# One tile and four fetches for the turned probabilities of a turn, keys fetched whole, and the residual's load behind the stores of q and k

## The chip, the cores and the metric

One NeuronCore of a Trainium2 chip runs the whole program. The metric is the device time of one execution in microseconds (us). The engines are TensorE (PE), VectorE (DVE), ScalarE (ACT), GpSimd (POOL) and SyncE (SP); each works through its own instructions in order, and semaphores hold an instruction back until what it reads or overwrites is ready. In this kernel SP issues every DMA.

## What is computed

Two layers of masked attention over 128 graphs of 128 nodes with 512 features each, in float32. Layer 0 has 4 heads, layer 1 has 8; each layer adds its output to its input and normalises.

```python
# layer 0: x (128, 128, 512), adj (128, 128, 128) of True and False
q, k, v = heads(x @ Wq), heads(x @ Wk), heads(x @ Wv)            # 4 heads of 64
attn = softmax(where(adj, q @ k.T * scale, -max))
x = layernorm(x + (attn @ v) @ Wo + bo)
# layer 1
h = layernorm(x) * gamma + beta
q, k, v = split(h @ w_qkv.T, 3)                                  # 8 heads of 64
attn = softmax(where(adj | eye, q @ k.T * scale, -1e9))
x = layernorm(x + (attn @ v) @ w_out.T + b_out)
```

## The kernel before

The 128 graphs go in 64 groups of 2. A loop of steps `step(s)` runs over the groups as a software pipeline: in step s the first layer's projections of group s are made, its scores and softmax for group s-1, its attention for group s-2, and of the second layer the q, k and v products of group s-3, the scores and softmax of s-4 and the attention and output of s-5. `opening`, `closing` and `last` fill and empty the pipeline. The order of all instructions is written out by hand in these functions; nothing reorders it. The matrix products use a seven-product scheme for 2 by 2 blocks (numbers 1 to 7 in the calls).

Softmax work of a step comes in three parts: part 0 is layer 0 (2 graphs of 4 heads), parts 1 and 2 are the two graphs of layer 1 (8 heads each). Each part is a tile of 128 by 1024 float32, 512 KB. `masked` fills it from the scores, `maxima`, `exps` and `normalised` make probabilities, with the last multiplication on POOL.

Several tensors have to be transposed over 128 partitions. VectorE transposes blocks of 32 by 32, and a trip through DRAM puts the blocks in place: `put` (or a direct store) writes the turned tile to a DRAM scratch, and `fetch` (L216 to L220) reads it back in four DMAs, one for each quarter of 32 partitions. These trips are:

- probabilities: `blocks` turns a part into `turnedp` (L604) and stores it to `scrp` (L214); `probs_arrive` fetches it into `pT`. There is one tile and one scratch per part, so 3 stores of 512 KB and 12 fetches of 128 KB in a step. `attend` of the next step multiplies with `pT` (L650).
- keys and queries of layer 1: `taken_tokens` adds up a product and turns it into `tk` or `tq` (L381), each in two halves, one per graph. Keys are stored by halves (L384, 256 KB each) and fetched by halves (`k_arrive`, 4 DMAs of 64 KB each); queries are stored once (L386, 512 KB) and fetched into `rawq` (`q_arrive`, 4 DMAs of 128 KB). `q_in_order` scales them into `qo` on ScalarE (L412). Scores of the next step read `kt` and `qo` (L536).
- the inputs of the two layers: `turn` and `arrive` (`turned`, `scr`, `raw0` and `raw`), one store of 512 KB and 4 fetches of 128 KB each.

The residual of a group is loaded a second time by `load_rows` (L80) into one of five buffers `r`, which the store of an earlier group's output (L719, in `norms`, called by `flush`) has to have left. The bias is added to it on POOL (`addend`, L671) before the output products are summed into it on VectorE (L502).

On SP, a step issues in this order: the next group's `x` and mask, `raw`, the output's store, the residual's load, the stores of part 0, of `turned`, and of part 1, the fetches of part 0, one half of the keys' store, the store of part 2, `raw0`, the fetches of part 1, the stores of q and of the other half of k, the first half of the keys' fetches, the fetches of part 2, the store of layer 1's `turned`, the q fetches, and the other half of the keys' fetches. Two `turned` buffers serve all five turns through DRAM of probabilities and inputs, so a turn waits for the store before the last.

Of the kernel before, what the change touches and what calls it, by code (L numbers as in the profile page):

```python
# [10 lines left out]
F32 = mybir.dt.float32  # L11
# [6 lines left out]
P = 128  # L18
# [9 lines left out]
def kernel(ctx: ExitStack, tc: tile.TileContext, x, adj, wq, wk, wv, wo, bo,  # L28
# [96 lines left out]

    w1 = const.tile([P, KC, 3 * INNER[1]], F32, name="w1")
    wo1 = const.tile([P, INNER[1] // P, E], F32, name="wo1")
    gb_raw = one.tile([2 * KC, P], F32, tag="pT1", name="gb_raw")
    gb = const.tile([P, 2 * KC], F32, name="gb")

    setup = []
# [79 lines left out]
    def put(t, name):  # L211

        scr = dram.tile(list(t.shape), F32, tag=name.split("_")[0], name=name)
        nc.sync.dma_start(scr, t)  # L214
        return scr

    def fetch(dst, scr):
        src = scr.rearrange("(a r) q x -> r q a x", r=32)
        for q in range(4):
            nc.sync.dma_start(dst[32 * q:32 * q + 32], src[:, q])  # L220
# [167 lines left out]
    def k_tile(g):  # L388
        KT[g] = one.tile([P, 4, G, K1, 32], F32, tag="kt", name=f"kt_{g}")
        return KT[g]  # L390
# [8 lines left out]
            RAW["q"] = one.tile([P, 4, G, K1, 32], F32, tag="raw", name=f"rawq_{g}")  # L399
            fetch(RAW["q"].rearrange("p a b c j -> p a (b c j)"), SCRQ["q"].rearrange("p q b x -> p q (b x)"))  # L400

    def k_arrive(g, b):

        if 0 <= g < NG and g not in PLAIN_QK:
            kt = KT[g] if b else k_tile(g)
            fetch(kt[:, :, b].rearrange("p a c j -> p a (c j)"), SCRQ["k"][:, :, b])

    def q_in_order(g):

# [67 lines left out]
    def out_product(l, g, *which):  # L477
        if not 0 <= g < NG:
            return
        aT = AT[l, g]  # L480
        hk = INNER[l] // P // 2
        w, ws = WO[l], WSO[l]
        EH = E // 2
        for i in which:
            sums_at = {3: 3, 5: 0, 6: 1, 7: 2}
            left = (SO[l, g][:, sums_at[i]] if i in sums_at else
                    {1: aT[:, 0, :hk], 2: aT[:, 0, hk:], 4: aT[:, 1, hk:]}[i])
            right = {1: w[:, :hk, :EH], 2: w[:, hk:, :EH], 3: w[:, hk:, EH:], 4: ws[:, 2],
                     5: w[:, :hk, EH:], 6: ws[:, 0], 7: ws[:, 1]}[i]
            bank, first = INTO[i]  # L490
            if first and bank == "c":
                ACC["o", bank] = mm_tile(f"oc{l}_{g}")
            elif first:
                ACC["o", bank] = ps_st.tile([P, 512], F32, tag=(bank, f"{bank}0")[l == 1 or g >= NG - 2],
                                          name=f"o{bank}{l}_{g}")
            acc = ACC["o", bank][:, :EH]
            for c in range(hk):
                nc.tensor.matmul(acc, left[:, c], right[:, c], start=first and c == 0, stop=c == hk - 1,  # L498
                                 skip_group_check=True)
            b, h = {1: (0, 0), 2: (0, 0), 6: (0, 1), 3: (0, 1), 5: (1, 1), 7: (1, 1), 4: (1, 0)}[i]  # L500
            part = R[g][:, b, h * EH:(h + 1) * EH]
            nc.vector.tensor_add(part, acc, part)  # L502
# [7 lines left out]
    def group_of(s, part):  # L510
        g = s - (4 if part else 1)
        return g if 0 <= g < NG else None
# [70 lines left out]
    def normalised(s, *parts):  # L583
        for part in parts:
            if group_of(s, part) is None:
# [3 lines left out]
            nc.gpsimd.tensor_tensor(SM[part], SM[part], rec[:, :, :, None].to_broadcast([P, 2, K1, N]),  # L589
                                    op=ALU.mult)  # L590

    def turned_tile(s, part):

        pT = PT[group_of(s, part), part] = one.tile([P, 4, 2 * K1, 32], F32, tag=f"pT{part}",
                                                    name=f"pT{part}_{s}")
        return pT

    def blocks(s, *parts):


        for part in parts:
            if group_of(s, part) is not None:
                t = one.tile([P, 4, 2 * K1 * 32], F32, tag="turned", bufs=2, name=f"turnedp{part}_{s}")
                nc.vector.transpose(t.rearrange("p q (h r) -> p q h r", r=32),  # L604
                                    SM.pop(part).rearrange("p i k (q r) -> p q (i k) r", r=32))
                SCR["p", part] = put(t, f"scrp{part}_{s}")

    def probs_arrive(s, *parts):
        for part in parts:
            if group_of(s, part) is not None:  # L610
                fetch(turned_tile(s, part).rearrange("p a h i -> p a (h i)"), SCR.pop(("p", part)))

    def blocks_direct(s, *parts):

# [196 lines left out]
    def step(s):  # L811

        made = scores(s)
        load_ahead(s + 1)
        if s > 2:
            in_order(s)
            sums(0, s)
        arrive(1, s - 3)
        masked(made, s, 0, 1, 2)
        attend(s)  # L820
        maxima(s, 0, 1)
        out_sums(0, s - 2)
        exps(s, 0, 0)
        product_0(s, 1)
        exps(s, 0, 1)
        out_product(0, s - 2, 1, 2, 5)
        maxima(s, 2)
        product_0(s, 2)
        normalised(s, 0)
        out_product(0, s - 2, 6, 3)  # L830
        exps(s, 1, 0)
        stats(1, s - 6, 0)
        stats(1, s - 6, 1)
        product_0(s, 6)
        exps(s, 1, 1)
        out_product(0, s - 2, 7)
        product_0(s, 5)
        out_product(0, s - 2, 4)
        flush()
        load_rows(s - 1)  # L840
        normalised(s, 1)
        finish(s - 3, 0)
        stats(0, s - 2, 0)
        stats(0, s - 2, 1)
        exps(s, 2, 0)
        blocks(s, 0)
        product_0(s, 7)
        finish(s - 3, 1)
        exps(s, 2, 1)
        product_0(s, 3)  # L850
        turn(0, s + 1)
        normalised(s, 2)
        product_0(s, 4)
        if s in (2, 3):
            prepare(len(setup) - (s == 2))
        blocks(s, 1)
        probs_arrive(s, 0)
        qk(s - 3, 1)
        if s == 2:
            weight_sums(w1qk, wsqk, 1)  # L860
            prepare(1)
        flush()
        qk(s - 3, 2)
        blocks(s, 2)
        arrive(0, s + 1)
        probs_arrive(s, 1)
        qk(s - 3, 6, 5)
        flush(latest)
        addend(1, s - 5)
        out_sums(1, s - 5)  # L870
        qk(s - 3, 7, 3, 4)
        k_arrive(s - 3, 0)
        probs_arrive(s, 2)
        turn(1, s - 2)
        out_product(1, s - 5, 1, 2)
        q_arrive(s - 3)
        v(s - 3, 1, 2)
        k_arrive(s - 3, 1)
        cleared(s + 1, 0, 1, 2)
        with_self(s - 2)  # L880
        out_product(1, s - 5, 6)
        v(s - 3, 6, 5)
        out_product(1, s - 5, 5)
        v(s - 3, 7, 3)
        out_product(1, s - 5, 7)
        q_in_order(s - 3)
        v(s - 3, 4)
        out_product(1, s - 5, 3, 4)
        addend(0, s - 1)
        if s == 2:  # L890
            weight_sums(w1v, wsv, 0, 1)
        if s == 3:
            weight_sums_out(1)

    def closing(s):

        made = scores(s)
        arrive(1, s - 3)
        masked(made, s, 0, 1, 2)
        attend(s)  # L900
        maxima(s, 0, 1)
        finish(s - 3, 0)
        out_sums(0, s - 2)
        if s == NG:
            stats(1, s - 6, 0)
            stats(1, s - 6, 1)
        exps(s, 0, 0)
        out_product(0, s - 2, 1, 2, 5)
        maxima(s, 2)
        flush()  # L910
        load_rows(s - 1)
        finish(s - 3, 1)
        qk(s - 3, 1)
        exps(s, 0, 1)
        out_product(0, s - 2, 6, 3)
        qk(s - 3, 2)
        normalised(s, 0)
        exps(s, 1, 0)
        out_product(0, s - 2, 7, 4)
        stats(0, s - 2, 0)  # L920
        stats(0, s - 2, 1)
        qk(s - 3, 6)
        exps(s, 1, 1)
        addend(1, s - 5)
        out_sums(1, s - 5)
        qk(s - 3, 5)
        normalised(s, 1)
        exps(s, 2, 0)
        blocks(s, 0)
        flush()  # L930
        qk(s - 3, 7)
        exps(s, 2, 1)
        turn(1, s - 2)
        blocks(s, 1)
        probs_arrive(s, 0)
        qk(s - 3, 3)
        normalised(s, 2)
        flush(latest)
        cleared(s + 1, 0, 1)
        qk(s - 3, 4)  # L940
        probs_arrive(s, 1)
        out_product(1, s - 5, 1, 2)
        k_arrive(s - 3, 0)
        q_arrive(s - 3)
        k_arrive(s - 3, 1)
        blocks(s, 2)
        if s < NG + 2:
            v(s - 3, 1)
        out_product(1, s - 5, 6, 5)
        if s < NG + 2:  # L950
            v(s - 3, 2, 6, 5)
        out_product(1, s - 5, 7)
        probs_arrive(s, 2)
        out_product(1, s - 5, 3, 4)
        q_in_order(s - 3)
        if s < NG + 2:
            v(s - 3, 7, 3, 4)
        stats(1, s - 5, 0)
        stats(1, s - 5, 1)
        cleared(s + 1, 2)  # L960
        addend(0, s - 1)
        with_self(s - 2)
# [78 lines left out]
```

## Time and profile before

| | |
|---|---|
| three runs | 3250.31, 3254.69, 3259.03 us; median 3254.69 |
| the profiled execution | 3262.01 us, with a span of 3260.2 us; granted TensorE clock 0.944 on average |
| DMA packets | 482,790, 570.93 MB, 175 GB/s on average |
| DMA engines | 59.8% of the span in packets of the queue that SP issues to |
| chain that ended last | PE 59%, DMA 17%, SP's queue 8%, DVE 7% of the span |

The span runs from the first to the last instruction on the chip; the time of an execution is a little longer. In the rows of the profile an instruction is named by its engine, its line in the kernel, its operation and the tiles it writes and reads (`out<-in`). PEld is the loading of weights into TensorE beside its products. "SPq" is SP's queue of DMA issues. The granted clock is the share of full speed that TensorE was allowed. The transfers that matter here, with their sizes and the median time from issue to landing:

```profile
scrp<-turnedp SPq DMA_DIRECT2D x189, 512.0 KB, 4.4
pT<-scrp SPq DMA_DIRECT2D x756, 128.0 KB, 3.8
r<-in_x_dram SPq DMA_DIRECT2D x63, 512.0 KB, 4.1
scrk<-tk SPq DMA_DIRECT2D x124, 256.0 KB, 3.6
scrq<-tq SPq DMA_DIRECT2D x62, 512.0 KB, 4.8
kt<-scrk SPq DMA_DIRECT2D x496, 64.0 KB, 3.7
rawq<-scrq SPq DMA_DIRECT2D x248, 128.0 KB, 4.1
```

### The profile page before, as it was taken

What the parts mean: (1) busy time and instruction counts of PE and PEld (TensorE: products, weight loads), DVE (VectorE), ACT (ScalarE), POOL (GpSimd) and SP (SyncE); (2) the same over time, 40 slices, a digit from 0 to 9 for tenths busy, and PEclk for the clock granted to TensorE, in tenths of its full rate; (3) what the DMA queues carried; (4) which work ended last, traced back from release to release, by engine and by line L of the source; (5) the groups of instructions that cost most, each with busy time, mean ns of one, the idle gap of its engine ahead of it and who ended that gap; (6) DMA issues with size and microseconds to landing.
All of it is one profiled execution on the core that took longest, in us unless ns stands there. A gap on an engine that the chain in (4) does not pass through costs nothing.

```text
span 3260.2 us, 54135 instructions
## 1 busy us (share of the span) xinstructions
PE 2918.0 (90%) x18077; PEld 2306.4 (71%) x18077; DVE 1931.4 (59%) x3545; ACT 1536.9 (47%) x4871; POOL 1744.8 (54%) x2311
## 2 busy tenths in 40 slices
PE   8899998898898988989899889889898998898987
PEld 8667767777677777676777767767777777677766
DVE  6566555566565555655656556556555566565554
ACT  3445445355454453544544535445445455354443
POOL 4455555564555555545556555555555564554553
PEclk9999999999999999999999999999999999999999
DMA  5565665655756656556566575565665665756642
GB/s 164 176 202 158 179 191 166 195 172 167 212 154 179 197 160 195 166 166 201 162 188 186 160 206 169 169 204 158 184 194 163 195 181 159 212 159 173 188 124 71
DMA packets 482790, 570.93 MB, mean 175 GB/s; under 512 B 60872, under 2 KB 383440, under 8 KB 482512
## 3 DMA queue, kind: packets, MB, share of 16 engines
q1 hardware_dynamic: 482512, 567.46, 59.8%
q8 instruction: 145, 2.38, 0.3%
q14 instruction: 133, 1.09, 0.1%
HBM read 304.09 MB, written 263.19 MB: 174 GB/s over the span
## 4 chain that ended last, share of the span: by engine, by line
PE 59%; DMA 17%; SPq 8%; DVE 7%; issue 5%; POOL 2%; ACT 2%; DVEq 0%; ACTq 0%; POOLq 0%
PE qka L338 10%; PE a L460 8%; DMA rawq<-scrq 7%; SPq L220 7%; PE av L650 6%; PE oa L498 6%; PE qkf L338 5%; PE sc L536 3%; PE va L338 3%; DMA scrp<-turnedp 3%; PE sc_a L536 3%; PE qkc L338 3%; PE of L498 3%; PE c L460 2%; PE f L460 2%
## 5 line engine op out<-in xcount | busy, mean ns | idle before, releaser
L302 POOL TENSOR_TENSOR xs<-xT 128x256 f32<-128x256 f32 x256 | 186.4, 728 | 835.9 <-ACT xT L256 695.0
L580 ACT ACTIVATE sm<-sm,nmax 128x128 f32<-128x128 f32 x1536 | 594.3, 391 | 5.5 <-DVE nmax L571 5.5
L589 POOL TENSOR_TENSOR sm<-sm,rec 128x1024 f32<-128x1024 f32 x192 | 364.1, 1896 | 279.6 <-DVE rec L588 273.7
L671 POOL TENSOR_TENSOR r<-r,bias 128x1024 f32<-128x1024 f32 x128 | 301.3, 2354 | 147.2 <-ACT r L670 147.2
L604 DVE STREAM_TRANSPOSE turnedp<-sm 128x1024 f32<-128x1024 f32 x189 | 231.7, 1226 | 200.9 <-DMA scrp<-turnedp 129.2
L412 ACT ACTIVATE qo<-rawq 128x512 f32<-128x512 f32 x124 | 71.2, 621 | 592.4 <-DMA rawq<-scrq 592.4
L502 DVE TENSOR_TENSOR r<-oa,r 128x256 f32<-128x256 f32 x508 | 207.9, 409 | 240.4 <-PE oa L498 123.3
L536 PE MATMUL sc_a<-kt,qo 64*128 64x128 f32 x512 | 125.2, 418 | 227.5 <-ACT qo L412 226.5
L580 ACT ACTIVATION_READ_ACCUMULATOR sm<-sm,nmax 128x1 f32 x1536 | 291.2, 190 | 0.0
L347 ACT COPY ev<-va 128x256 f32<-128x256 f32 x128 | 47.6, 372 | 512.1 <-PE va L338 512.1
L536 PEld LDWEIGHTS sc_a<-kt,qo 64*128 64x128 f32 x512 | 107.1, 307 | 240.0 <-ACT qo L412 238.6
L502 DVE TENSOR_TENSOR r<-of,r 128x256 f32<-128x256 f32 x254 | 107.3, 423 | 216.6 <-PE of L498 209.9
L338 PE MATMUL qkf<-w,xs 128*128 128x512 f32 x496 | 233.2, 592 | 0.5 <-ACT eqk L347 0.5
L338 PE MATMUL qka<-wsqk,xs 128*128 128x512 f32 x496 | 233.1, 592 | 0.0
L571 DVE TENSOR_REDUCE nmax<-sm 128x8 f32<-128x1024 f32 x192 | 226.4, 1205 | 0.2
L498 PE MATMUL oa<-wso,so 128*128 128x256 f32 x760 | 208.6, 384 | 11.0 <-DVE r L502 6.3
L565 DVE COPY_PREDICATED sm<-m,sc 128x512 f32<-128x512 uint8 x256 | 171.5, 723 | 64.6 <-PE sc L531 45.3
L498 PE MATMUL of<-wo,so 128*128 128x256 f32 x760 | 208.3, 383 | 0.8 <-POOL so L302 0.7
L565 DVE COPY_PREDICATED sm<-m,sc_a 128x512 f32<-128x512 uint8 x64 | 46.8, 732 | 267.4 <-PE sc_f L536 254.2
L716 ACT ACTIVATE r<-r,shift,root 128x512 f32<-128x512 f32 x254 | 193.0, 808 | 23.4 <-POOL shift L705 23.4
L302 POOL TENSOR_TENSOR so<-aT 128x256 f32<-128x256 f32 (+1 forms) x254 | 150.2, 591 | 75.5 <-ACT aT L653 75.5
L338 PEld LDWEIGHTS qkf<-w,xs 128*128 128x128 f32 x496 | 94.2, 190 | 119.5 <-issue 117.7
(178 smaller groups left out, 7300.0 us busy)
## 6 DMA issues: line engine op xcount, KB each, us to landing
scrp<-turnedp SPq DMA_DIRECT2D x189, 512.0 KB, 4.4
pT<-scrp SPq DMA_DIRECT2D x756, 128.0 KB, 3.8
scr<-turned SPq DMA_DIRECT2D x125, 512.0 KB, 4.2
raw<-scr SPq DMA_DIRECT2D x500, 128.0 KB, 3.8
r<-in_x_dram SPq DMA_DIRECT2D x63, 512.0 KB, 4.1
out_dram<-r SPq DMA_DIRECT2D x63, 512.0 KB, 2.8
scrk<-tk SPq DMA_DIRECT2D x124, 256.0 KB, 3.6
scrq<-tq SPq DMA_DIRECT2D x62, 512.0 KB, 4.8
```

Of the source, the lines that this page charges most:

```text
L220: nc.sync.dma_start(dst[32 * q:32 * q + 32], src[:, q])
L302: nc.gpsimd.tensor_tensor(o, a0, a1, op=op)
L338: nc.tensor.matmul(o, lhsT, rhs, start=first and m == 0, stop=m == len(todo) - 1, skip_group_check=True)
L460: nc.tensor.matmul(acc[:, at * P:(at + 1) * P], lhsT, rhs, start=first and n == 0, stop=n == len(todo) - 1, skip_group_check=True)
L498: nc.tensor.matmul(acc, left[:, c], right[:, c], start=first and c == 0, stop=c == hk - 1, skip_group_check=True)
L502: nc.vector.tensor_add(part, acc, part)
L536: nc.tensor.matmul(ps[h % 2][:, h // 2, :].rearrange("p (a j) -> p a j", j=32), QO[g, b][r, h // 2], keys_of(g, b, h // 2, r), start=True, ...
L571: nc.vector.tensor_reduce(NMAX[part], SM[part], AX.X, ALU.max, negate=True)
L580: nc.scalar.activation(sm[:, i, k, :], sm[:, i, k, :], AF.Exp, bias=nmax[:, i, k:k + 1], accum_out=total[:, i, k:k + 1])
L589: nc.gpsimd.tensor_tensor(SM[part], SM[part], rec[:, :, :, None].to_broadcast([P, 2, K1, N]), op=ALU.mult)
L604: nc.vector.transpose(t.rearrange("p q (h r) -> p q h r", r=32), SM.pop(part).rearrange("p i k (q r) -> p q (i k) r", r=32))
L671: nc.gpsimd.tensor_tensor(R[g], R[g], (bias0, bias1)[l][:, None, :].to_broadcast([P, G, E]), op=ALU.add)
```

## The change

The three parts of a step share one `pT` tile and one DRAM scratch, in which the 3 parts of a row's quarter lie side by side. Each part is still stored on its own; all that a step has are fetched together in four DMAs of up to 384 KB. The keys are fetched whole, in four DMAs of 128 KB behind the q fetches, instead of by halves. In `step`, the store of part 0 is put ahead of the output's store, and the residual's load behind the stores of q and k; the normalisation of part 2 moves behind the turn of part 1. In `closing`, all probabilities are fetched at the place where part 2's were. A small setup tile takes another tile's buffer, since `pT1` is gone.

```diff
-    gb_raw = one.tile([2 * KC, P], F32, tag="pT1", name="gb_raw")
+    gb_raw = one.tile([2 * KC, P], F32, tag="sm2", name="gb_raw")
...
-    def k_arrive(g, b):
+    def k_arrive(g):
 
         if 0 <= g < NG and g not in PLAIN_QK:
-            kt = KT[g] if b else k_tile(g)
-            fetch(kt[:, :, b].rearrange("p a c j -> p a (c j)"), SCRQ["k"][:, :, b])
+            fetch(k_tile(g).rearrange("p a b c j -> p a (b c j)"), SCRQ["k"].rearrange("p q b x -> p q (b x)"))
...
+    PALL, SCRP = {}, {}
+
     def turned_tile(s, part):
 
-        pT = PT[group_of(s, part), part] = one.tile([P, 4, 2 * K1, 32], F32, tag=f"pT{part}",
-                                                    name=f"pT{part}_{s}")
+        if s not in PALL:
+            PALL[s] = one.tile([P, 4, 3, 2 * K1, 32], F32, tag="pT", name=f"pT_{s}")
+        pT = PT[group_of(s, part), part] = PALL[s][:, :, part]
         return pT
...
-                SCR["p", part] = put(t, f"scrp{part}_{s}")
+                if s not in SCRP:
+                    SCRP[s] = dram.tile([P, 4, 3, 2 * K1 * 32], F32, tag="scrp", name=f"scrp_{s}")
+                nc.sync.dma_start(SCRP[s][:, :, part], t)
 
     def probs_arrive(s, *parts):
-        for part in parts:
-            if group_of(s, part) is not None:
-                fetch(turned_tile(s, part).rearrange("p a h i -> p a (h i)"), SCR.pop(("p", part)))
+        parts = [p for p in parts if group_of(s, p) is not None]
+        if parts:
+            for part in parts:
+                turned_tile(s, part)
+            lo, hi = parts[0], parts[-1] + 1
+            fetch(PALL[s][:, :, lo:hi].rearrange("p a t h i -> p a (t h i)"),
+                  SCRP[s][:, :, lo:hi].rearrange("p q t x -> p q (t x)"))
...
@@ step(s)
         out_product(0, s - 2, 4)
+        normalised(s, 1)
+        blocks(s, 0)
         flush()
-        load_rows(s - 1)
-        normalised(s, 1)
         finish(s - 3, 0)
...
-        blocks(s, 0)
         product_0(s, 7)
...
-        normalised(s, 2)
         product_0(s, 4)
...
         blocks(s, 1)
-        probs_arrive(s, 0)
+        normalised(s, 2)
         qk(s - 3, 1)
...
         arrive(0, s + 1)
-        probs_arrive(s, 1)
         qk(s - 3, 6, 5)
...
         qk(s - 3, 7, 3, 4)
-        k_arrive(s - 3, 0)
-        probs_arrive(s, 2)
+        load_rows(s - 1)
+        probs_arrive(s, 0, 1, 2)
         turn(1, s - 2)
         out_product(1, s - 5, 1, 2)
         q_arrive(s - 3)
         v(s - 3, 1, 2)
-        k_arrive(s - 3, 1)
+        k_arrive(s - 3)
...
@@ closing(s)
         blocks(s, 1)
-        probs_arrive(s, 0)
...
-        probs_arrive(s, 1)
         out_product(1, s - 5, 1, 2)
-        k_arrive(s - 3, 0)
         q_arrive(s - 3)
-        k_arrive(s - 3, 1)
+        k_arrive(s - 3)
         blocks(s, 2)
...
-        probs_arrive(s, 2)
+        probs_arrive(s, 0, 1, 2)
         out_product(1, s - 5, 3, 4)
```

## The prediction

> **What bounds the kernel now.** I read the totals first, then the list of who TensorE (PE) waited for, then one step of the SP queue in order of time, then short windows with the transfer rate.
>
> ```profile
> span 3260.2 us, 54135 instructions
> PE 2918.0 (90%) x18077; PEld 2306.4 (71%) x18077; DVE 1931.4 (59%) x3545; ACT 1536.9 (47%) x4871; POOL 1744.8 (54%) x2311
> ```
>
> ```profile
> PE sc_a L536 <- ACT qo L412: 226.5, 59, 5.1
> PE a L460 <- DVE qkv L474: 68.8, 62, 1.5
> PE av L650 <- DMA pT<-scrp: 8.2, 4, 3.0
> ```
>
> PE is busy 90% of the span, and of the 342 us that it idles, 226.5 lie in one place, once per step (59 times, 3.84 us each): the first layer-1 score product of a step waits for the scaled queries qo (us in total, times, longest). A step is about 50 us. The 68.8 us at L460 wait for VectorE sums whose order the change leaves as it was. So only the qo wait can move much. Its release, in the SP queue (start, duration, engine, line, operation):
>
> ```profile
> 1634.31 1.80 SPq L220 DMA_DIRECT2D pT<-scrp  x4
> 1636.21 0.38 SPq L386 DMA_DIRECT2D scrq<-tq  x1
> 1636.71 0.52 SPq L384 DMA_DIRECT2D scrk<-tk  x1
> 1637.27 3.21 SPq L220 DMA_DIRECT2D kt<-scrk  x4
> 1640.59 2.01 SPq L220 DMA_DIRECT2D pT<-scrp  x4
> 1642.70 0.37 SPq L214 DMA_DIRECT2D scr<-turned  x1
> 1643.17 2.19 SPq L220 DMA_DIRECT2D rawq<-scrq  x4
> 1645.41 2.09 SPq L220 DMA_DIRECT2D kt<-scrk  x4
> ```
>
> and beside it what VectorE (DVE) and PE did, from their own orders of time:
>
> ```profile
> 1632.51 0.71 DVE L381 STREAM_TRANSPOSE tq<-eqk 128x512 f32<-128x512 f32 x1
> ```
>
> ```profile
> 1645.48 1.16 PE L531 MATMUL sc<-qkv 64*128 64x128 f32 x16
> 1650.31 0.58 PE L536 MATMUL sc_a<-kt,qo 64*128 64x128 f32 x1 [3.67 <-ACT qo L412]
> ```
>
> The turned queries tq are ready at 1633.22, but their store is issued only at 1636.21, because SP is still issuing older fetches. The last q fetch starts at 1644.89, lands near 1649.5, ACT scales (0.64), PE starts at 1650.31: **17.1 us after tq is ready**. PE has run out of other work at 1646.64, **13.4 us** after tq. The wait is the difference, and the forecast needs one number: what becomes of 17.1.
>
> The rates decide that (window, its length, busy time and count of PE, PEld, DVE, ACT, POOL, granted clock, DMA share, GB/s):
>
> ```profile
> 5.00:8.00 3.00, 2.46 (x11) 1.94 (x10) 0.69 (x1) 0.83 (x2) 1.60 (x3) 1.00 1.08 295
> 21.00:25.00 4.00, 4.00 (x43) 3.71 (x41) 2.82 (x4) 1.36 (x3) 2.30 (x4) 1.00 1.05 399
> 1625.00:1626.50 1.50, 1.50 (x5) 0.64 (x4) 0.12 (x1) 0.47 (x1) 1.50 (x1) 1.00 1.02 418
> 1635.00:1638.00 3.00, 3.00 (x15) 2.64 (x14) 2.08 (x6) 0.37 (x1) 3.00 (x4) 1.00 1.05 224
> 1607.00:1617.00 10.00, 10.00 (x82) 9.47 (x79) 6.42 (x17) 8.61 (x38) 4.54 (x9) 1.00 0.00 0
> ```
>
> All but the last are at a DMA share of about 1, so the DMA engines are full in each. Loads into all 128 partitions run at 399 GB/s (2 KB pieces) and 295 (weights, 512 B pieces); stores from 128 partitions at 418; but the fetches, each into 32 partitions in 1 KB pieces, at 224. Small pieces alone do not explain that, since 512 B pieces reach 295. Two more fetch windows give 233 (3184.5 to 3187) and 236 (1646 to 1649); the best single microsecond is 273. Meanwhile, early in the step (1607 to 1617), nothing moves at all.
>
> **The change, part by part.** *Removed:* 8 of the 12 pT issues and 4 of the 8 kt issues per step, about 0.45 us each on SP, so 5.4 us of SP time. Without them SP reaches the q store in time: its last work before is the raw0 fetch, issued as soon as scr0 has landed and scrp2 is stored, about 1628 to 1631. The q store then goes at 1633.3 instead of 1636.2. That is 2.9 us won.
>
> *Moved into the tail:* the same bytes of pT now all lie between the k store and the q fetch: before, 4 fetches of 128 KB were there, now 4 of 384 KB, 1.57 MB in all. The residual's load (512 KB) is there too, and k's whole fetch is behind q's, where PE needs all of it for the first two products. Counting landings from the issue of the q store (each transfer after the first costs its bytes by its rate, since they queue):
> - q store, alone: 2.61 and 3.08 are what scrp stores took from issue to landing where nothing else ran (chain of waits at 3208.95 and 3139.42); 2.85.
> - k store, 262 KB at 295 (the 512 B row): 0.89. Residual, 524 KB at 399: 1.31.
> - pT, 1,573 KB at 224: **7.02**.
> - scr1 store, 524 KB at 418: 1.25.
> - q fetch, 524 KB at 224: 2.34; k fetch, the same: 2.34.
>
> Sum 18.0 us, where 17.1 stood. q is there at 15.7 and scaled by 16.4, so k's landing takes the place of q as what ends the wait. SP doesn't bound this: 16 issues at 0.47 are 7.5 us, and even where an issue waits for the transfer eight before it to land (the built program asks that), the last k fetch goes when scr1 has landed, at 13.3, and needs some 3 us. PE's wait grows by 0.9 us a step.
>
> *The rate is the unshown term.* No row has a 384 KB fetch in 3 KB pieces. Bounds: 399 as the wide loads (pT 3.94, sum 14.9) and 216, the slowest fetch window (1598 to 1600; pT 7.28, q and k 2.43 each, sum 18.4). I take 224, since destination (32 partitions), source and queue are those of the fetch rows and only the piece grows. The residual's load can cost more than its share: alone it lands 4.1 us after its issue, 0.6 later than the sum has it. With a first store of 3.08 and the slowest rate that makes 19.3, so +2.2 at the upper end.
>
> The Trainium skill speaks on both sides here. "DMA: Bandwidth & Descriptors", rules for kernel authors, says to merge many small transfers into a large one; that would put pT nearer 399 and the sum near 14.9. "SBUF — State Buffer", the DMA port swizzle, says that partitions 0 to 31 reach only 8 of 16 ports, measured there as 189 GB/s at 1 MiB with a limit of 218, whatever the piece; by 218 the sum would be 18.3. The 224 of this trace, half of 418, agrees with the second.
>
> *Parts at nothing.* The scrp stores become 512 pieces of 1 KB instead of 128 of 4 KB: between 1.25 us (418) and 1.78 (295) each, in the stretch from 1618 to 1630, where the DMA share is 0.29 to 1.06, 0.64 on average; that slack covers it, 0.5 us each without it. turnedp0 goes ahead of two statistics on DVE (1.23 us later); the POOL chain of 1.56 us behind them then starts at 1619.4 instead of 1618.7 and ends at 1621.0, before POOL's next work at 1621.75. The out store has scrp0 ahead of it on SP; nobody waits for it but the residual, which moves later. Residual: lands about 5 to 6 us after tq, 1638.3 to 1639; the bias add on POOL (1638.27, 2.35 us) waits up to 1 us, and POOL is idle from 1640.6 to the next step. pT lands 12.1 us after tq, 6 us ahead of its use. The reciprocal behind turnedp1 still waits for ACT until 1623.2. gb_raw's other place: used once, at the start.
>
> *Clock.* After each wait PE runs at a lower granted clock: the same products take 6.3 to 7.8 us at a granted clock of 0.60 to 0.75 (1500.7 to 1508.5, 1601 to 1607.5), and 4.9 at 1.00 in the step at 3095.5, the one with no wait. Longer waits fall among the 7.6 to 7.8 more often: half the steps by 0.6 us, +0.3 a step.
>
> *Sum.* (0.91 + 0.3) x 58 steps = 70. The step that ends at 3095.5 has no wait now (its q store left SP at once, 13.3 us before): it would get 4.7 plus about 2 of clock, +7. In the closing steps all probabilities now arrive in the last place: 4.7, 2.3 and 2.3 us more fetching at three places where PE already waits for pT (5.6 us); I take 6 of these 9. Together **+83 us**. The profiled execution took 3262.01 us (span 3260.2), so 3345; the median of the runs is 7.3 lower, so 3338.
>
> **Rivals.**
> 1. *pT runs at the wide rate.* For it: bigger pieces, less per piece. Against: 224 in 1 KB pieces beside 295 in 512 B pieces. Sum 14.9, -2.2 a step, and up to 1 us of clock: 13 - 2.2 x 58 is -115, with clock -173; 3080 to 3140, 3110. It decides from 6.1 us for pT (258 GB/s) downward: below that the kernel is faster.
> 2. *Between:* pieces of 3 KB help some, 240 to 290 GB/s; pT 6.6 to 5.4, the step moves +0.4 to -0.9 us; 3210 to 3285, no change in the middle.
> 3. *Worse:* the residual's latency and the slow rate both count, +2.2 and 0.4 of clock: 3254.7 + 13 + 150 = 3418.
> 4. *Nothing moves,* as bytes are the same and only issues fall: then 3255. Against: PE's wait is fed by the very tail whose order changes.
>
> **How the numbers follow.** Forecast 0.70 (own range 3285 to 3395), rival 1 0.14, 2 and 4 together 0.11, 3 0.05. A measurement of this kernel tells 0.3% (10 us) from no change. Slower: 0.70 and 0.05, less 0.04 at the forecast's lower edge, plus 0.02 of the cases between, 0.73. The 0.13 that is left beside rival 1 gives 0.05 to no change and 0.08 to faster, 0.22 with rival 1. The range leaves out most of rival 1 and of 3: 3180 to 3395.
>
> **What would show it.** SP issues scrq within 0.5 us of tq's end; pT takes 9 us and more from issue to landing; fetch windows stay at 215 to 240 GB/s; PE's wait at L536 is put down to kt<-scrk, not to qo, with 270 to 300 us over 60 places. Wrong if windows of pT alone show over 260 GB/s, or if the wait shrinks.

## The result, and the profile after

| | before | after |
|---|---|---|
| median of the runs | 3254.02 us (3250.31 to 3259.03) | 3428.91 us (3424.05 to 3431.28) |
| ratio | | 1.0535, 95% interval 1.0516 to 1.0553 |
| span of the profiled execution | 3260.2 us | 3427.0 us |
| granted TensorE clock, mean | 0.944 | 0.922 |

The kernel became slower, as forecast, but by 175 us where 83 were forecast; 3429 lies outside the range (3180 to 3395) and next to rival 3 (3418). The list of who PE waited for, after (us in total, times, longest):

```profile
PE sc_a L535 <- ACT qo L411: 292.1, 54, 10.0
PE a L459 <- DVE qkv L473: 68.9, 62, 1.5
PE sc_a L535 <- DMA kt<-scrk: 41.0, 7, 7.0
PE sc_f L535 <- DMA kt<-scrk: 24.0, 60, 0.9
PE av L658 <- DMA pT<-scrp: 12.9, 2, 6.6
```

The wait at the first layer-1 score product (L535, L536 before) has grown from 226.5 to 333 us, and a new one of 24 us has come to the product after it, sc_f. One step of the SP queue after:

```profile
1665.64 0.34 SPq L386 DMA_DIRECT2D scrq<-tq  x1
1666.64 0.52 SPq L384 DMA_DIRECT2D scrk<-tk  x1
1667.21 0.65 SPq L80 DMA_DIRECT2D r<-in_x_dram  x1
1667.95 1.92 SPq L220 DMA_DIRECT2D pT<-scrp  x4
1669.97 0.47 SPq L214 DMA_DIRECT2D scr<-turned  x1
1670.54 4.68 SPq L220 DMA_DIRECT2D rawq<-scrq  x4
1676.77 4.48 SPq L220 DMA_DIRECT2D kt<-scrk  x4
```

and PE and the turn of q in the same step:

```profile
1677.87 1.16 PE L530 MATMUL sc<-qkv 64*128 64x128 f32 x16
1684.59 0.76 PE L535 MATMUL sc_a<-kt,qo 64*128 64x128 f32 x2 [5.56 <-ACT qo L411]
1685.82 0.58 PE L535 MATMUL sc_f<-kt,qo 64*128 64x128 f32 x1 [0.46 <-DMA kt<-scrk]
```

```profile
1664.90 0.71 DVE L381 STREAM_TRANSPOSE tq<-eqk 128x512 f32<-128x512 f32 x1
```

q's store leaves SP 0.03 us after tq is ready (1665.61), so the backlog on SP is gone as forecast. But PE starts at 1684.59, 19.0 us after tq, where 17.1 stood; PE had nothing left to do at 1679.0. The transfers' own table shows why (size, median from issue to landing):

```profile
pT<-scrp SPq DMA_DIRECT2D x244, 384.0 KB, 6.8
r<-in_x_dram SPq DMA_DIRECT2D x63, 512.0 KB, 4.3
scrq<-tq SPq DMA_DIRECT2D x62, 512.0 KB, 2.7
rawq<-scrq SPq DMA_DIRECT2D x248, 128.0 KB, 10.4
kt<-scrk SPq DMA_DIRECT2D x248, 128.0 KB, 5.6
```

A q fetch that took 4.1 us from issue to landing takes 10.4: it stands in line behind the probabilities. And a window of 7 us with almost nothing but pT runs at the fetch rate, with the DMA engines full (share 1.05, 213 GB/s in the last columns):

```profile
1671.00:1678.00 7.00, 7.00 (x35) 5.89 (x35) 2.15 (x6) 0.74 (x2) 2.35 (x1) 1.00 1.05 213
```

Where the 166.8 us between the two spans came from: 54 steps in the middle became 2.38 us longer each (128.4), the stretch up to the sixth step's score product 24.6, and what follows the 54 steps 13.8. In all runs below, a step splits into three: the wait at sc_a, the stretch from sc_a to the last attention product (av), and the rest, which is the same 39.0 to 39.2 us everywhere. Means over 53 steps of the trace, in us:

| run | wait at sc_a | sc_a to end of av | of it at half clock | step | median, us |
|---|---|---|---|---|---|
| before | 3.85 | 7.07 | 4.69 | 50.1 | 3254 |
| after | 5.42 | 7.94 | 5.35 | 52.5 | 3429 |
| e1, residual back | 4.01 | 8.01 | 5.45 | 51.2 | 3353 |
| e2, probabilities last | 0.00 | 12.42 | 6.50 | 51.5 | 3366 |
| e3, twelve small fetches | 5.08 | 7.99 | 5.42 | 52.2 | 3402 |
| e5, only k whole | 3.24 | 8.28 | 5.85 | 50.7 | 3298 |
| e6, only residual late | 2.57 | 6.46 | 3.34 | 48.2 | 3153 |
| e7, q and k before part 2 | 1.61 | 7.78 | 4.10 | 48.6 | 3172 |
| e8, arranged by the sum | 0.00 | 4.78 | 0.00 | 43.8 | 2899 |
| e9, parts 0 and 1 early | 1.80 | 7.72 | 4.08 | 48.7 | 3191 |
| e10, e8 with 0 and 1 merged | 0.18 | 6.02 | 0.19 | 45.3 | 2995 |

### The profile page after: what moved, and what is told of

Read it like the earlier page. It is cut to its first block, busy times and chain, and to the rows that moved or that the text cites. A ratio compares the mean times of both kernels' runs of the same rounds, so it can differ in the third digit from the quotient of the medians.

```text
span 3427.0 us, 53191 instructions
## 1 busy us (share of the span) xinstructions
PE 2948.2 (86%) x18077; PEld 2324.5 (68%) x18077; DVE 1945.9 (57%) x3545; ACT 1538.5 (45%) x4871; POOL 1750.7 (51%) x2311
## 4 chain that ended last, share of the span: by engine, by line
PE 59%; DMA 28%; DVE 8%; issue 2%; POOL 2%; ACT 1%; SPq 0%; DVEq 0%; POOLq 0%; ACTq 0%
DMA scr<-turned 18%; PE qka L338 12%; DMA kt<-scrk 9%; PE a L459 8%; PE qkf L338 6%; PE av L658 6%; PE oa L497 5%; PE sc_f L535 4%; PE qkc L338 3%; PE sc L535 3%; PE f L459 2%; PE c L459 2%; PE oc L497 2%; DVE st L690 2%; DVE turnedp L606 2%
## 5 line engine op out<-in xcount | busy, mean ns | idle before, releaser
L535 PE MATMUL sc_a<-kt,qo 64*128 64x128 f32 x512 | 150.1, 445 | 333.6 <-ACT qo L411 292.1
L535 PEld LDWEIGHTS sc_a<-kt,qo 64*128 64x128 f32 x512 | 115.5, 312 | 344.7 <-ACT qo L411 343.0
L497 PE MATMUL oa<-wso,so 128*128 128x256 f32 x760 | 209.9, 386 | 12.1 <-DVE r L501 7.4
L661 ACT COPY aT<-av 128x512 f32<-128x512 f32 x64 | 37.5, 586 | 323.2 <-PE av L658 323.2
```

The costliest lines, as they stand in the source:

```text
L535: nc.tensor.matmul(ps[h % 2][:, h // 2, :].rearrange("p (a j) -> p a j", j=32), QO[g, b][r, h // 2], keys_of(g, b, h // 2, r), start=True, ...
```

## The experiments

The median of before was 3253.77 beside e1 to e4, 3267.15 beside e5 to e8 and 3253.33 beside e9 and e10; the ratios are each against their own.

**e1, the residual's load back at its old place.**

```diff
         blocks(s, 0)
         flush()
+        load_rows(s - 1)
...
-        load_rows(s - 1)
         probs_arrive(s, 0, 1, 2)
```

> The changed kernel with the residual's load put back behind the first flush of a step (it waits there for the output's store, as before); all else as changed. Theory 1 (everything behind q's store lands one after the other, and the sum of the landings sets PE's wait): the residual took 2.07 us of that line (k's store lands 14.92 us before the next sc_a, the residual 12.85), so the wait of 5.4 us at sc_a falls to about 3.4 and a step from 52.6 to about 50.3: 3295 us, 3265 to 3325. Theory 2 (the residual's load is hidden beside the stores and only the pT fetches count): no change, 3415 to 3440.

Measured 3353.33 us, ratio 1.0307 (1.0290 to 1.0324): 76 us below the change, of 134 expected, and 28 above theory 1's range. Theory 2 falls. But the line got only 1.5 us shorter: without the residual it is the first pT fetch that lands late, 2.8 us behind k's store, where a quarter otherwise takes 1.9. At this place the first load behind the stores costs 0.7 to 1.0 us beyond its bytes, whichever load it is, and that cost stayed in the line. It isn't so behind every store: in the changed kernel the first q fetch landed 0.70 us behind scr1's store, the others 0.62 apart.

**e2, probabilities behind q and k.**

```diff
-        probs_arrive(s, 0, 1, 2)
         turn(1, s - 2)
...
         k_arrive(s - 3)
+        probs_arrive(s, 0, 1, 2)
```

> The changed kernel with the one fetch of all probabilities put behind the fetches of q and k; the residual's load stays where the change has it. Theory 1 (order in the line decides): q lands about 9.5 us and k about 12 us after q's store is issued, PE is free 13.4 us after it, so PE's wait for qo and kt goes to nearly nothing; pT then lands at about 19.9 us and is needed at about 15.8, so a new wait of some 4 us stands at the attention products (av). Net per step 1.5 to 2.5 us won on the changed kernel: 3310 us, 3270 to 3350. Theory 2 (the amount of bytes in the tail decides, in whatever order): no change, 3415 to 3440.

Measured 3365.83 us, ratio 1.0343 (1.0324 to 1.0363).

```profile
PE av L658 <- DMA pT<-scrp: 328.4, 62, 10.3
...
PE sc_f L535 <- DMA kt<-scrk: 10.9, 20, 0.9
...
PE sc_a L535 <- ACT qo L411: 5.4, 2, 2.7
```

The wait for q and k all but vanished (5.4 and 10.9 us in all) and a wait for the last probabilities took its place, 5.3 us a step where 4 were expected: the attention products come 2.0 us after the scores begin (medians) and not 2.4, and pT landed 20.4 us after q's store was issued (19.9 expected). So the time lies 16 us above theory 1's range, and below theory 2's. Order decides which product waits; where 1.57 MB stand in the tail, one of them does.

**e3, twelve fetches of 128 KB at the same place.**

```diff
-                if s not in SCRP:
-                    SCRP[s] = dram.tile([P, 4, 3, 2 * K1 * 32], F32, tag="scrp", name=f"scrp_{s}")
-                nc.sync.dma_start(SCRP[s][:, :, part], t)
+                SCR["p", part] = put(t, f"scrp{part}_{s}")
...
-            lo, hi = parts[0], parts[-1] + 1
-            fetch(PALL[s][:, :, lo:hi].rearrange("p a t h i -> p a (t h i)"),
-                  SCRP[s][:, :, lo:hi].rearrange("p q t x -> p q (t x)"))
+            for part in parts:
+                fetch(PALL[s][:, :, part].rearrange("p a h i -> p a (h i)"), SCR.pop(("p", part)))
```

> The changed kernel with a DRAM scratch for each part and twelve fetches of 128 KB (1 KB pieces), all at the same place as the four of 384 KB. Theory 1 (bytes into 32 partitions set the cost, not the count or size of fetches): the same line, pT 7.0 to 7.8 us, so 3390 to 3435. Theory 2 (the size of the fetches is the harm, since 3 KB pieces or few large transfers run worse): pT far cheaper, 3280 to 3340. Theory 3 (SP's issues are the bound, and merging is what helps): eight more issues of 0.47 us, 3.8 us a step slower, 3600 and above.

Measured 3401.75 us, ratio 1.0455 (1.0433 to 1.0478). Theory 1: eight more issues and pieces of a third of the size change 27 us of 175, and to the better. The merging that gave the change its name is neither help nor main harm; the place is.

**e4, the disputed rate by itself.** Behind the end of the changed kernel, three times: loads of x into a tile of 128 partitions, the same pieces either by quarters or wide.

```diff
+    def alone():
+        for n in range(3):
+            for kind in ("quarters", "wide"):
+                for width in (768, 256):
+                    t = one.tile([P, 4 * width], F32, tag="pT", name=f"{kind}{width}")
+                    flat = x[6 * n:6 * n + 6].rearrange("b n e -> (b n e)")[:P * 4 * width]
...
+                        src = flat.rearrange("(a r q w) -> r q a w", a=4, r=32, w=width)
+                        for q in range(4):
+                            nc.sync.dma_start(dst[32 * q:32 * q + 32], src[:, q])
...
+                        src = flat.rearrange("(r q w) -> r q w", r=P, w=width)
+                        for q in range(4):
+                            nc.sync.dma_start(t[:, q * width:(q + 1) * width], src[:, q])
```

> The changed kernel with 48 loads from x behind its end, where no other transfer runs; their data are not used. Three times: four fetches into 32 partitions each with 3 KB pieces, the same with 1 KB pieces, four loads of the same bytes into 128 partitions with 3 KB pieces (the same 128 pieces at the same distances in DRAM), the same with 1 KB pieces. Theory 1 (32 partitions at a time are the limit): landings of the 384 KB fetches 1.75 to 1.85 us apart (about 218 GB/s), of the wide ones about 1.0 us (390 GB/s). Theory 2 (the reading of pieces a few KB apart in DRAM, or the piece size, is the limit): both alike.

Landings of the third and fourth 384 KB fetch of a set, read from the trace:

```
quarters  3433.43 3435.24 | 3457.53 3459.37 | 3482.05 3483.88   1.81, 1.84, 1.83 us apart: 215 GB/s
wide      3444.84 3445.78 | 3469.49 3470.42 | 3493.39 3494.32   0.94, 0.93, 0.93 us apart: 421 GB/s
```

Same bytes, same 3 KB pieces at the same distance in DRAM: into 32 partitions at a time they take twice as long. The 128 KB fetches in 1 KB pieces landed 0.60 us apart into 32 partitions, which is the same rate (218 GB/s); the wide ones of that size landed 0.49 us apart, about as fast as SP issued them (0.45), so they show no rate. Theory 1, from one execution in which each set stands three times. "SBUF — State Buffer" of the Trainium skill, in the section on the DMA port swizzle, gives a limit of 218 GB/s for partitions 0 to 31; the 215 of this run, for partitions 64 to 95 and 96 to 127, agrees.

**e5, e6, e7: parts of the change, and of its reverse, on the kernel before.** e5 has k whole behind q; e6 only the residual's load behind the stores of q and k; e7 has k whole and part 2's fetch behind it. `k_whole(g)` fetches the keys as `k_arrive(g)` of the changed kernel does.

```diff
 e5
-        k_arrive(s - 3, 0)
...
-        k_arrive(s - 3, 1)
+        k_whole(s - 3)
...
 e6
         flush()
-        load_rows(s - 1)
...
         qk(s - 3, 7, 3, 4)
+        load_rows(s - 1)
         k_arrive(s - 3, 0)
...
 e7, beside e5
-        probs_arrive(s, 2)
         turn(1, s - 2)
...
         k_whole(s - 3)
+        probs_arrive(s, 2)
```

> The kernel before with one part of the change alone: k fetched whole, in four DMAs of 128 KB, behind the q fetches. Theory 1 (the sum of the landings): q lands 1.4 us earlier, as the first halves of k no longer lie ahead of it, and k's second quarter, which the first product needs, 1.2 us behind q, the last one 2.4 us behind: about even, 3254 us, 3225 to 3285, with part of PE's wait put down to kt<-scrk. Theory 2 (fetching k whole is a main cause of the loss): 3300 and above.

> The kernel before with the residual's load behind the stores of q and k, as in the change, and nothing else. Theory 1 (two effects of opposite sign): SP no longer waits for the output's store at that place, so the store of part 0 goes some 3 us earlier, DVE's second turn no longer waits for it, and q's store goes when tq is ready; that takes up to 3 us out of the wait; the residual itself adds 2.07 us ahead of q. Sum after q's store: 2.7 + 1.05 + 2.07 + 1.4 (half of k) + 2.34 (part 2) + 1.25 + 2.34 = 13.2, and 13.9 with the scaling, where 17.1 stood: nearly the whole wait gone, 2960 to 3100. Theory 2 (only the place in the line counts, a backlog on SP does not): 2.07 us a step slower, 3370 to 3390.

> The kernel before with k fetched whole and the fetch of part 2 put behind the fetches of q and k; residual, parts 0 and 1 as before. Theory 1 (what lies ahead of q in the line is what PE waits for): q lands 3.6 us earlier and is scaled 13.4 us after tq, k's last quarter lands at about 15.1, part 2 at 17.5 where av needs it at about 16; waits of some 2.5 us a step in all instead of 3.8 and a higher granted clock: 3110 us, 3050 to 3180. Theory 2 (bytes, not order): 3240 to 3270.

e5: 3298.32 us, ratio 1.0098 (1.0083 to 1.0113), 13 us past the slow end of what theory 1 had and 2 short of theory 2. The kernel before took 3267 beside it, and against that the loss is 31 us, the edge of theory 1. q came earlier and the wait at sc_a fell by 0.6 us, but the products after it took 1.2 us more: sc_a and sc_f alternate, so the last quarter of k, which sc_f needs, holds up both. Half of the 1.2 is the clock (5.85 us at half clock for 4.69), the other half k.

e6: 3152.63 us, ratio 0.9654 (0.9633 to 0.9675). The residual's move alone is a gain of 3.5%. Before, VectorE waited 129 us in total for the first store of probabilities, which stood on SP behind the residual's load and its wait for the output's store. These are the lines of the kernel before:

```profile
SPq L80 <- DMA out_dram<-r: 144.4, 59, 3.1
DVE turnedp L604 <- DMA scrp<-turnedp: 129.2, 42, 4.2
```

In e6 this wait of VectorE is down to 1.1 us in all, and q's store leaves SP 0.08 us after tq (median; 0.30 on average) where 3.45 stood, with every fetch still issued as before. The time is 53 us above theory 1's range; theory 1 had the sign, half of the gain, and four tenths of the wait that it promised to take away: q's store landed 4.9 us after its issue, not 2.7, since raw0 and part 1 still filled the line in front of it.

e7: 3172.27 us, ratio 0.9703 (0.9683 to 0.9723); expected 3110, and within its bounds. Here it is again k's last quarter that took the rest (sc_f waits 43.3 us for it).

**e8, arranged by the sum.**

```diff
+        normalised(s, 1)
+        blocks(s, 0)
         flush()
-        load_rows(s - 1)
-        normalised(s, 1)
...
-        blocks(s, 0)
...
-        normalised(s, 2)
...
         blocks(s, 1)
+        load_rows(s - 1)
+        normalised(s, 2)
         probs_arrive(s, 0)
...
-        k_arrive(s - 3, 0)
-        probs_arrive(s, 2)
         turn(1, s - 2)
         out_product(1, s - 5, 1, 2)
         q_arrive(s - 3)
         v(s - 3, 1, 2)
-        k_arrive(s - 3, 1)
+        k_whole(s - 3)
+        probs_arrive(s, 2)
```

> A version made by the same sum. From the kernel before: store of part 0 ahead of the output's store (as in the change), the residual's load behind the store of part 1, parts 0 and 1 fetched at their old places, before tq is ready; then q's store, k's store, layer 1's turned store, q's fetch, k's fetch whole, and part 2's fetch last. Theory 1: q lands 9 to 10 us after its store, k about 12, part 2 about 14.5, all before PE needs them (13.4, 13.4 and 15.1), so no wait at sc_a and no lowered clock; a step falls to 45.4 to 46.5 us: 2960 us, 2930 to 3030. Theory 2 (bytes, not order): 3200 and above.

Measured **2899.07 us, ratio 0.8876 (0.8863 to 0.8889)**, better than expected (below the range). After the issue of q's store, q landed at 9.7 us, k at 12.2 and part 2 at 14.6 (medians), as the sum had it. A step takes 43.8 us where 45.4 to 46.5 were expected; what the estimate had too high was not looked into. PE is busy 96% of the span and the granted clock is 0.991:

```profile
span 2901.3 us, 54119 instructions
...
PE 2778.8 (96%) x18077; PEld 2180.1 (75%) x18077; DVE 1933.0 (67%) x3545; ACT 1538.7 (53%) x4871; POOL 1745.6 (60%) x2311
```

```profile
PE a L465 <- DVE qkv L479: 68.5, 62, 1.5
...
PE av L655 <- DMA pT<-scrp: 6.0, 3, 2.6
...
PE sc_a L541 <- ACT qo L417: 2.6, 1, 2.6
```

**e9, the change with parts 0 and 1 fetched early; e10, e8 with parts 0 and 1 merged.**

```diff
 e9, beside the change
         normalised(s, 2)
+        probs_arrive(s, 0)
...
         arrive(0, s + 1)
+        probs_arrive(s, 1)
...
-        probs_arrive(s, 0, 1, 2)
+        probs_arrive(s, 2)
...
 e10, beside e8, with the change's shared tile and scratch
-        probs_arrive(s, 0)
...
-        probs_arrive(s, 1)
+        probs_arrive(s, 0, 1)
```

> The changed kernel with one part undone: parts 0 and 1 are fetched on their own at their old places, before q's store (from the shared scratch into the shared tile); part 2, the residual, and k whole stay as the change has them. Theory 1 (1.05 MB of probabilities moved in between q's store and q's fetch are the main cause of the loss, against which the residual's move is a gain): line after q's store 4.9 + 0.7 + 2.3 + 2.4 + 1.25 + 2.4 = 13.9 us to q, 15.1 to the quarter of k that the first product needs; PE waits 1.7 us a step and the products after it take about 7.5: a step of 48.4 us, 3165 us, 3130 to 3205, well below the kernel before. Theory 2 (the shared scratch, the 1 KB stores or k are what makes the change slow): 3300 and above.

> The version of e8 with the shared scratch and tile of the change, and parts 0 and 1 fetched together in four DMAs of 256 KB at part 1's place. Theory 1 (what decides is when the line of transfers is empty; merging makes part 0 wait for part 1): 2.4 us more ahead of q's store; q still in time, k's last quarter about 1 us and part 2 about 2 us late: 2900 + 58 x (1 to 2 and some clock) = 2990 us, 2940 to 3060. Theory 2 (fewer, larger fetches help, or cost nothing, once the order is right): 2870 to 2915.

e9: 3190.85 us, ratio 0.9794 (0.9759 to 0.9829). With this one part undone, the change becomes a gain: 238 us below it, and 62 below the kernel before. q landed 13.9 us after its store was issued and k's second quarter at 15.0 (13.9 and 15.1 expected). e10: 2995.07 us, ratio 0.9202 (0.9181 to 0.9223), 96 us above e8's time: merging costs what waiting for the later part costs, even in the good arrangement. q's store landed 7.2 us after its issue where e8 has 4.8, which is the 2.4 us more ahead of it that were expected. The shared scratch by itself was not put into e8.

## Why the prediction was right and wrong

*What bounds the kernel:* right. Only the stretch from tq to the end of av moved in any run, and the rest of a step stayed at 39.0 to 39.2 us.

*The mechanism:* right in what fills the line. The q store left SP at once, the pT bytes took its gain and more, fetch windows stayed at 213 to 230 GB/s, and e4 shows the rate is that of 32 partitions. e9 shows that these bytes in the tail, parts 0 and 1, are worth 238 us, so more than the whole loss. e3 shows that the number and size of the fetches are not the cause: twelve small ones at the same place cost 27 us less.

*Why q's store left at once:* not shown as the working has it, and luck in part. It put the gain down to the issues that go away. But in e6, e8 and e9 all eight fetches of parts 0 and 1 are still issued ahead of q's store, and it leaves 0.03 to 0.08 us after tq (medians); so they did not have to go. What these runs share is that the store of part 0 no longer stands behind the residual's wait for the output's store. The changed kernel has both, and no run has fewer issues ahead of q's store and nothing else.

*The residual's move:* a gain of 115 us on the kernel before (e6), a loss of 76 in the changed one (e1). What it gains before is that wait ahead of part 0's store. In the changed kernel part 0's store is ahead of it already, and in e1 q's store still leaves 0.03 us after tq; there the load only lengthens the line.

*The sum: wrong in size.* The step that failed is "Sum 18.0 us, where 17.1 stood", with "PE's wait grows by 0.9 us a step" behind it. Landings after the issue of q's store (medians of 54 steps), in us:

| | forecast | measured |
|---|---|---|
| q's store | 2.85 | 2.7 |
| k's store | 3.74 | 3.8 |
| residual | 5.05 | 5.8 |
| last pT fetch | 12.1 | 13.4 |
| scr1 store | 13.3 | 14.8 |
| last q fetch | 15.7 | 17.4 |
| last k fetch | 18.0 | 19.8 |

Two terms carry most of the 1.8 us. The residual was put at its bytes by its rate (1.31) and took 2.0: it lands 4.3 us after its own issue (4.1 in the kernel before), later than its turn in the line, and the 0.6 of this that the working named was left to the upper bound. The four pT fetches took 7.6 us where 7.02 were put: 1.9 a quarter, though the same fetch alone takes 1.83 and the rate of 224 gave 1.755. The terms behind them are each 0.1 to 0.2 too small. Why the fetches are slower inside the kernel than alone was not tried.

*What ends the wait:* right, though the list hides it. In 52 of 53 steps k's second quarter lands after the first scaled q is ready, and PE begins 0.14 us behind it (median). In the step shown, the first scaled q was ready at 1684.06, k's second quarter landed at 1684.46 and PE began at 1684.59. The list still puts 292 us to qo and 65 to kt. But what the working made of it fell short: PE does not stand until all of k is there. The sc_a products read k's first two quarters and the sc_f products the last two. So PE begins with the second quarter and then stops short until the last, so that sc_f comes 1.15 us after sc_a, where 0.10 stood before. So the wait itself grew by 1.57 us a step (0.9 forecast), and the products behind it by 0.87, where only the clock was priced, at 0.3. The clock was sized right: the time at half clock grew from 4.69 to 5.35 us, which costs half of the 0.66, 0.33 us. The other 0.5 is the waiting for the rest of k, a term that the working put at nothing. The table bears this out. With e8's 4.78 and half of the time at half clock, the kernel before and e6, which fetch k by halves, come out within 0.1 us of what they took; e5 is 0.6 over, and e10, with hardly any half clock, 1.1.

*Two of the signs:* "pT takes 9 us and more from issue to landing" failed (6.8 median, though the last quarter took 10.1 in the step shown), and so did the wait under kt instead of qo, for the reason above.

*Parts at nothing and the ends:* the step without a wait before got 6.1 us (7 forecast), the closing ones 7.7 more (6 forecast). The first steps weren't priced apart and took 24.6 us; the waits at their first three score products went from 6.8 to 19.5 us in sum.

Together: the two profiled executions are 167 us apart where 83 were forecast. Of these 84 us, +2.38 a step instead of +1.21 over the 54 middle steps is 63 and the first steps are 20. (The medians are 175 apart, as the profiled execution of the kernel before was 8 us above its median.) Rival 3 had the right two causes, the residual's lead and a slower rate, at a chance of 0.05. Its size was right by luck in part: it had +2.2 of wait and 0.4 of clock, where 1.57 of wait, 0.33 of clock and 0.5 for the rest of k came, and it hadn't priced the first steps. The lead had been measured in this very trace (4.1 us from issue to landing against 1.3 by bytes) and belonged in the likeliest sum.

## What to carry to other kernels

Where transfers queue in one line, write down the landing of each behind the one whose data the bottleneck engine awaits: what is needed first goes first, and what can go before the line fills, goes early; in these runs the number of issues made little difference (e3), the place in the line much. A fetch merged over several sources starts when the last of them is ready, and takes the idle time of the DMA engines that the earlier ones used. Give a load behind stores its whole time from issue to landing where that ends later than its turn in the line, and price a product that needs four fetches by the last of them. Before crediting a queue's delay to the number of its issues, look for the instruction in it that waits.

## What the runs showed of the hardware

- 384 KB into 32 partitions at a time take 1.83 us, into 128 partitions 0.93 us (e4), with the same pieces.
- A wait of PE costs more than itself. The products from sc_a to the end of av take 4.78 us with no wait (e8) and 7.07 after one of 3.85 us (before), at a granted clock of 0.5 for 4.7 of them. So of the 6.3 us that a step lost against e8, 2.3 are the products behind the wait. The wait need not be long: in e7, 51 of 53 steps ran 3.41 or 6.83 us at half clock, behind waits of 0.86 to 2.76 us at sc_a (1.6 to 3.3 us with those just behind it). "TensorE: Matmul & The Clock Gate" of the Trainium skill, in its part on the clock gate, gives a window of 3.41 us; nearly all stretches of half clock in these traces last 3.41, 6.83 or 10.24 us.
- Eight transfers in flight can hold over 2 MB: in the step shown SP issues the last q fetch only when the first pT fetch, eight before it, has landed. q's fetches took 10.4 us from issue to landing (median, up to 11.8), and SP waited 362 us in all for pT to land; q's and k's fetches still landed 0.6 us apart.
